# Fifth list tiles of two experts in one stage of TensorE: 96 rows each, on column groups

## The chip, the cores and the metric

The kernel runs on one core of a Trainium2 chip. The metric is the device time of one execution in microseconds (us), the lower the better. All arithmetic is in 32-bit floats (f32). The engines are TensorE (PE, matrix products; its weight loads are listed apart as PEld), VectorE (DVE), ScalarE (ACT), GpSimd (POOL) and SyncE (SP, which issues most plain DMAs).

## The reference

Two layers on 1024 tokens of 1024 channels: group norm, a convolution-attention hybrid and a residual sum; then layer norm, causal attention of 16 heads and a residual sum; then layer norm and a mixture of eight experts with a residual sum. The change lies in the mixture alone:

```python
gate_logits = jax.nn.softmax(x @ gate_w + gate_b, axis=-1)
selected = (gate_logits >= THRESHOLD).astype(x.dtype)          # THRESHOLD = 0.1
weights = gate_logits * selected
weights = weights / jnp.where(wsum == 0, jnp.ones_like(wsum), wsum)   # wsum: sum over experts
for e in range(E):                                             # E = 8
    out = out + weights[:, e:e + 1] * (x @ expert_w[e] + expert_b[e])
```

A token counts for an expert only where its gate is at least 0.1. The reference, run on its inputs, selects 560, 592, 542, 569, 578, 552, 545 and 538 of the 1024 tokens for experts 0 to 7.

## The kernel before

**Lists.** While attention's output is projected, each token's gates are computed, and each expert gets a list of its selected tokens (`place`, `enter`, `read_lists`). The list's entries are read 128 at a time, called list tiles. `gather`, `slot` and `add` hold the token numbers and gates. For experts 1 to 6 five list tiles are always worked off, 640 entries (`SLOTS`, L61). Experts 0 and 7 (`SHORT`, L62) have four, from lists without the last 128 tokens; the last 128 tokens go through these two experts densely (`dense` and `last_pe`). After all this a branch (L1219) handles what longer lists hold; its condition is `most_i > SLOTS`, where `most_i` is the largest list, and for experts 0 and 7 their list plus 128 (`last_lists`, L1006).

**One list tile.** `get` (L1060, through `fetch`) gathers its rows with four indirect DMAs issued by POOL, of 256 channels each. `put` (L1063, through `turn`) transposes them on DVE, so that channels lie on partitions, as TensorE's stationary operand needs. The result is scaled by the gate on ACT and added to the output by an indirect DMA issued by POOL (`add_rows`, L743).

**Four tiles in two pairs.** `products` (L1079) takes two list tiles, 256 rows, against a 1024 x 1024 expert matrix by Strassen's scheme in Winograd's form: seven block products, each of four f32 matmuls with 128 x 128 stationary blocks and 512 moving columns. `row_sums` forms the sums of row blocks (`sums_of_A`, L147), and `first_sum`, `second_sum`, `third_sum` (L1048) and `fourth_sum` form those of the weights. `third_sum` overwrites the block b12 of the expert's weights in place. The seven products alternate between two groups of three PSUM banks (`mm`, `tr`), and DVE takes each out.

**The fifth tile.** `left_over` (L1117) multiplies one list tile by the expert's weights directly: for each of two halves of the columns, eight f32 matmuls of a full 128 x 128 stationary block (`weighted`, L731, the matmul on L737). It stands ahead of the expert's products.

**Order.** From L1152 on the order is written out by hand. For each expert: `left_over` (1 to 6 only), then `load(e + 1)` (the next expert's weights, two DMAs on SP), then `products` for pair 0 and pair 1. Both take a dictionary `between`: other engines' work that is issued after product n of the seven. Weights of even and odd experts have buffers of their own (`w_even`, `w_odd`), so an expert's weights load during the one before it.

Of the kernel before, what the change touches and what calls it, by code (L numbers as in the profile page):

```python
# [28 lines left out]
F32 = mybir.dt.float32  # L32
# [6 lines left out]
P = 128  # L39
# [18 lines left out]
NEG = -1e29  # L58
THRESHOLD = 0.1
Q = 4  # L60
SLOTS = 5 * P  # L61
SHORT = (0, E - 1)  # L62


# [1 line left out]
def kernel(  # L66
# [80 lines left out]
    def sums_of_A(a11, a12, a21, a22, s1, s2, s4):  # L147
        nc.vector.tensor_add(s1, a21, a22)
        nc.vector.tensor_sub(s2, s1, a11)
        nc.vector.tensor_sub(s4, a12, s2)  # L150
        nc.vector.tensor_sub(a21, a11, a21)

    def layer_norm(ln, t, dst):

# [300 lines left out]
    with ExitStack() as attention:  # L455
# [20 lines left out]
        def sums_of_B():  # L476
            nc.vector.tensor_sub(T[0], b12, b11)
            nc.vector.tensor_sub(T[1], b22, T[0])
            nc.vector.tensor_sub(b12, b22, b12)
            nc.vector.tensor_sub(T[2], b21, T[1])  # L480

        n_products = 0
# [221 lines left out]

        return w_tile(f"{name}{e}_{r}", expert_w[e][:, ts(r, HALF)], home=home)

    def expert_bias(e, home, name="w_e"):
        bias = home.tile([P, C], F32, tag="bias", name=f"{name}_bias{e}", bufs=1)
        nc.sync.dma_start(bias, expert_b[e].partition_broadcast(P))
        return bias  # L710

    def fetch(e, k, home, name="w_e", bufs=None):

        row = home.tile([P, Q, C // Q], F32, tag="xg", name=f"{name}_xg{e}_{k}", bufs=bufs)
        for g in range(Q):
            nc.gpsimd.indirect_dma_start(  # L716
                out=row[:, g, :],
                out_offset=None,
                in_=table[: (TOK - P) * Q, :] if e in SHORT else table,
                in_offset=bass.IndirectOffsetOnAxis(ap=gather[:, e, k * Q + g : k * Q + g + 1], axis=0),  # L720
            )
        return row

    def turn(row_T, row):

        nc.vector.transpose(  # L726
            row_T.rearrange("p c (g j) -> p g c j", g=Q),
            row.rearrange("p g (c i) -> p g c i", c=NC),
        )

    def weighted(gate, row_T, w, bias, home, name, between={}):  # L731
# [8 lines left out]
            nc.scalar.mul(y[:, ts(j, HALF)], y[:, ts(j, HALF)], gate)  # L740
        return y

    def add_rows(e, k, y):  # L743
        nc.gpsimd.indirect_dma_start(  # L744
            out=out[: TOK - P, :] if e in SHORT else out,
            out_offset=bass.IndirectOffsetOnAxis(ap=add[:, e, k : k + 1], axis=0),
            in_=y,
            in_offset=None,
            compute_op=ALU.add,
        )  # L750

    def by_rows(e, tiles, w, bias, home, name):

        tiles = list(tiles)

        def turned(k, row):
            row_T = home.tile([P, NC, P], F32, tag="row_T", name=f"{name}_xg_T{e}_{k}", bufs=3)
            turn(row_T, row)
            return row_T

        fetched = [fetch(e, k, home, name) for k in tiles[:2]]
        ready = [turned(tiles[0], fetched[0])]
        for n, k in enumerate(tiles):
            if n + 2 < len(tiles):
                fetched.append(fetch(e, tiles[n + 2], home, name))
            if n + 1 < len(tiles):
                ready.append(turned(tiles[n + 1], fetched[n + 1]))
            add_rows(e, k, weighted(slot[:, e, 1, k : k + 1], ready[n], w, bias, home, f"{name}{e}_{k}"))

    with ExitStack() as gating:  # L770
        l2, l2w = pool(gating, "l2"), pool(gating, "l2w", 2)
# [234 lines left out]
        def last_lists(entries):  # L1006
            read_lists(1, E, entries)


            pn = tr("pn")  # L1010
            nc.tensor.matmul(pn[:, :E], ones, kept, start=True, stop=True)
            need = l2.tile([P, E], F32, tag="need", name="need")
            nc.vector.tensor_copy(need, pn[:, :E])
            pn0 = tr("pn0")
            nc.tensor.matmul(pn0[:, :2], ones, kept_short, start=True, stop=True)
            nc.vector.tensor_scalar(need[:, :: E - 1], pn0[:, :2], float(P), None, ALU.add)
            most = l2.tile([P, 1], F32, tag="most", name="most")
            nc.vector.tensor_reduce(most, need, AX.X, ALU.max)
            nc.vector.tensor_copy(most_i, most)
# [11 lines left out]
        def half(e, j, l):  # L1031
            return w[e][l][:, 4 * j : 4 * j + 4, :]
# [15 lines left out]
        def third_sum(e):  # L1048

            T3[e] = half(e, 0, 1)  # L1050
            if e == E - 1:
                free = w_even.tile([P, NC, HALF], F32, tag="w", name="free")
                T3[e] = free[:, : NC // 2, :]
                last_rows.append(free[:, NC // 2 : NC // 2 + 2, :].rearrange("p a b -> p (a b)"))
            nc.vector.tensor_sub(T3[e], half(e, 1, 1), half(e, 0, 1))

        row = {}
        last = SLOTS // P - 1

        def get(e, k):  # L1060
            row[e, k] = fetch(e, k, two, bufs=3)

        def put(e, k):  # L1063

            if k == last:
                A[e, k] = l2w.tile([P, NC, P], F32, tag="row_T", name=f"one{e}", bufs=3)
                turn(A[e, k], row[e, k])
            else:
                pair, i = divmod(k, 2)
                if i == 0:  # L1070
                    A[e, pair] = two.tile([P, 2, NC, P], F32, tag="A", name=f"A{e}_{pair}")
                turn(A[e, pair][:, i, :, :], row[e, k])
# [6 lines left out]
        def products(e, pair, between):  # L1079
# [34 lines left out]
            rows_out(1, 0)  # L1114
            add_rows(e, 2 * pair + 1, y[1])

        def left_over(e):  # L1117

            between = {0: lambda: (fourth_sum(e), put(e, 1), get(e, 3)), 1: lambda: row_sums(e, 0)}
            get(e, 2)  # L1120
            y = weighted(slot[:, e, 1, last : last + 1], A[e, last], w[e], bias[e], l2w, f"one{e}", between)
            add_rows(e, last, y)

        with tc.manual_schedule():
# [23 lines left out]
            )  # L1150
            get(0, 3)
            for e in range(E):  # L1152
                if e not in SHORT:
                    left_over(e)
                if e + 1 < E:
                    load(e + 1)
# [6 lines left out]
                if e == 0:  # L1163
                    between[2] = lambda: (stage(3, NT - 1), fourth_sum(0), put(0, 2))
                    between[3] = lambda: (entries.append(copy_lists(1)), put(0, 3))
                    between[4] = lambda: (last_lists(entries[0]), row_sums(0, 1))
                    between.pop(1)
                elif e == E - 1:
                    between[0] = lambda: (third_sum(e), get(e, 3))
                    between[1] = lambda: (fourth_sum(e), put(e, 2))  # L1170
                if e + 1 < E - 1:
                    between[5] = lambda: get(e + 1, last)
                    between[6] = lambda: get(e + 1, 0)
                elif e + 1 == E - 1:
                    between[5] = lambda: get(e + 1, 0)
                    between[6] = lambda: get(e + 1, 1)
                products(e, 0, between)
                between = {}
                if e + 1 < E - 1:
                    between = {  # L1180
                        1: lambda: (bias.update({e + 1: expert_bias(e + 1, l2w)}), put(e + 1, last)),
                        2: lambda: (put(e + 1, 0), get(e + 1, 1)),
                        4: lambda: first_sum(e + 1),
                        5: lambda: second_sum(e + 1),
                        6: lambda: bias_step(e + 1),
                    }
                elif e + 1 == E - 1:
                    between = {
                        1: lambda: (bias.update({e + 1: expert_bias(e + 1, l2w)}), put(e + 1, 0), get(e + 1, 2)),
                        2: lambda: put(e + 1, 1),  # L1190
                        3: lambda: row_sums(e + 1, 0),
                        4: lambda: first_sum(e + 1),
                        5: lambda: second_sum(e + 1),
                        6: lambda: bias_step(e + 1),
                    }
                else:
                    between = {
                        1: lambda: nc.sync.dma_start(last_rows[0], out[ts(NT - 1, P), :]),
                        4: lambda: nc.vector.scalar_tensor_tensor(
                            last_rows[0], bias[e], gated[NT - 1][0][:, e, 1:2], last_rows[0], ALU.mult, ALU.add  # L1200
                        ),
                    }
# [16 lines left out]
    with tc.If(count > SLOTS), ExitStack() as rest:  # L1219
        w_rest, l3 = pool(rest, "w_rest", 4), pool(rest, "l3", 3)  # L1220
        for e in range(E):
            w_e = [half_weights(e, r, w_rest, "w_r") for r in range(2)]
            tiles = range(SLOTS // P - 1, NT - 1) if e in SHORT else range(SLOTS // P, NT)
            by_rows(e, tiles, w_e, expert_bias(e, l3, "w_r"), l3, "w_r")


# [57 lines left out]
```

## Time and profile before

| | us |
|---|---|
| median of 3 runs | 1311.58 |
| lowest and highest | 1308.51, 1311.72 |
| the profiled execution | 1310.25 |
| its span, first to last instruction | 1308.4 |
| PE busy | 1286.6 |
| DVE busy | 664.3 |
| POOL busy | 344.3 |
| ACT busy | 245.3 |
| DVE add of 128 x 512 (L1101) | 0.691 |
| DVE transpose of one list tile (L726) | 1.241 |
| POOL gather, one of four of a list tile (L716) | 1.048 |
| DMA of half an expert's weights, issue to landing | 12.1 |

A row of a group reads: source line, engine, operation, what is written <- what is read, shape of the stationary block (partitions x columns, with a star), shape of the output, count | busy time in us, mean ns of one | idle time of the engine before them, and what ended it. A row of the timeline or of the chain begins with the start in us from the span's start and the length in us. Matmul records overlap each other, since the next one enters while the last one leaves; so the distance of starts is what a matmul costs, and not its length. An f32 matmul leaves two records. The line numbers are those of the kernel before.

### The profile page before, as it was taken

To read this page: it belongs to the slowest core of one execution; us is meant where nothing else is said; L and a number is where in the kernel's file an instruction comes from. 1 tells how busy PE (TensorE), PEld (TensorE's weight loads), DVE (VectorE), ACT (ScalarE), POOL (GpSimd) and SP (SyncE) were. 2 spreads that over 40 slices of the span, in tenths; PEclk is the share of its full clock that TensorE was granted. 3 is DMA by queue.
4 is the path that set the end of the run, shared out by engine and by line. 5 is a ranking of instruction groups with operands and counts; after the bars stand their busy time and mean duration, and the time that the engine had idled before them with its cause. 6 is when DMAs were issued, how large, how long until landed. Compare 5 with 4: busy or idle time off the path is not lost.

```text
span 1308.4 us, 12324 instructions
## 1 busy us (share of the span) xinstructions
PE 1286.6 (98%) x4550; PEld 695.5 (53%) x4550; DVE 664.3 (51%) x1250; ACT 245.3 (19%) x572; POOL 344.3 (26%) x365
## 2 busy tenths in 40 slices
PE   9999999998999999999999998999999999999998
PEld 5445894777884555555554544444444444444443
DVE  5874220566323555554444755655646465555642
ACT  3200111330001333333323322111111111110110
POOL 0000060230000211111111113445454544453530
PEclk9999999998999999999999998999999999999999
DMA  9020023512201202010505215374757566555532
GB/s 350 2 65 17 1 76 92 203 65 81 65 18 46 65 1 65 1 65 1 193 17 196 96 65 201 73 220 115 214 124 190 147 164 174 145 165 140 111 75 58
DMA packets 61042, 136.12 MB, mean 104 GB/s; under 512 B 5905, under 2 KB 20257, under 8 KB 60977
## 3 DMA queue, kind: packets, MB, share of 16 engines
q1 hardware_dynamic: 47664, 94.32, 20.7%
q0 software_dynamic: 13312, 40.96, 14.4%
q8 instruction: 38, 0.62, 0.2%
q14 instruction: 28, 0.22, 0.1%
HBM read 97.51 MB, written 33.55 MB: 100 GB/s over the span
## 4 chain that ended last, share of the span: by engine, by line
PE 93%; DVE 4%; POOL 1%; DMA 1%; issue 1%; ACT 0%; DVEq 0%; ACTq 0%; POOLq 0%
PE p L1093 28%; PE pqk L489 15%; PE po L646 8%; PE pq L257 7%; PE pv L489 7%; PE one_pe L737 6%; PE pT L376 3%; PE py L441 2%; PE pk L319 2%; PE pc L340 2%; PE pv L401 2%; PE sc L573 2%; PE pst L617 2%; PE pa L627 2%; PE last_pe L1209 1%; POOL w_e_xg L716 1%
## 5 line engine op out<-in xcount | busy, mean ns | idle before, releaser
L716 POOL DMA_INDIRECT w_e_xg<-rows,gather x152 | 159.2, 1048 | 69.1 <-issue 42.0
L1093 PE MATMUL p<-w_e,A 128*128 128x512 f32 x368 | 164.6, 597 | 1.8 <-DVE slot L954 1.8
L605 POOL TENSOR_TENSOR s<-s,total 128x256 f32<-128x256 f32 x64 | 51.5, 826 | 346.4 <-DVE total L602 338.4
L1093 PEld LDWEIGHTS p<-w_e,A 128*128 128x128 f32 x368 | 70.4, 192 | 90.5 <-issue 88.6
L646 PE MATMUL po<-w_p,y_T 128*128 128x512 f32 x256 | 116.1, 598 | 0.0
L744 POOL DMA_INDIRECT out_dram<-y,add x32 | 60.8, 1899 | 205.7 <-ACT y L1099 133.1
L1093 PE MATMUL p<-T,S 128*128 128x512 f32 x256 | 112.7, 592 | 0.0
L1099 ACT ACTIVATE y<-y,slot 128x512 f32<-128x512 f32 x64 | 46.2, 722 | 341.3 <-DVE y L1107 172.5
L257 PE MATMUL pq<-w_q,xn 128*128 128x512 f32 x224 | 99.6, 596 | 1.4 <-DVE q_s L261 1.1
L489 PE MATMUL pqk<-ln,w_qk 128*128 128x512 f32 x192 | 85.0, 592 | 0.0
L737 PE MATMUL one_pe<-w_e,one 128*128 128x512 f32 x192 | 83.4, 592 | 0.0
L1093 PEld LDWEIGHTS p<-T,S 128*128 128x128 f32 x256 | 48.6, 190 | 60.8 <-issue 60.7
L646 PEld LDWEIGHTS po<-w_p,y_T 128*128 128x128 f32 x256 | 46.3, 190 | 49.1 <-issue 48.7
L257 PEld LDWEIGHTS pq<-w_q,xn 128*128 128x128 f32 x224 | 41.8, 190 | 51.8 <-issue 47.4
L726 DVE STREAM_TRANSPOSE A<-w_e_xg 128x1024 f32<-128x1024 f32 x32 | 39.7, 1241 | 51.4 <-DMA w_e_xg<-rows,gather 51.4
L737 PEld LDWEIGHTS one_pe<-w_e,one 128*128 128x128 f32 x192 | 36.5, 190 | 45.9 <-issue 45.7
L595 ACT ACTIVATE s<-s,top 128x256 f32<-128x256 f32 (+1 forms) x128 | 56.6, 443 | 18.1 <-DVE top L593 18.0
L489 PEld LDWEIGHTS pqk<-ln,w_qk 128*128 128x128 f32 x192 | 35.9, 190 | 42.1 <-issue 41.1
L489 PE MATMUL pqk<-T,S_qk 128*128 128x512 f32 x128 | 57.7, 593 | 0.0
L1093 PE MATMUL p<-w_e,S 128*128 128x512 f32 x128 | 57.5, 592 | 0.0
L1093 PE MATMUL p<-T,A 128*128 128x512 f32 x128 | 57.5, 592 | 0.0
L618 ACT COPY s_T<-pst 128x384 f32<-128x384 f32 x64 | 27.5, 481 | 157.6 <-PE pst L617 157.6
(256 smaller groups left out, 1801.0 us busy)
## 6 DMA issues: line engine op xcount, KB each, us to landing
w_e<-in_expert_w_dram SPq DMA_DIRECT2D x16, 2048.0 KB, 12.1
w_qk<-in_W_attnT_dram SPq DMA_DIRECT2D x8, 1024.0 KB, 6.4
xn<-in_xT_dram SPq DMA_DIRECT2D x8, 512.0 KB, 7.8
x_at<-in_x_dram SPq DMA_DIRECT2D x8, 512.0 KB, 7.1
w_v<-in_W_attnT_dram SPq DMA_DIRECT2D x2, 2048.0 KB, 11.8
x_rows<-x_at SPq DMA_DIRECT2D x8, 512.0 KB, 2.7
w_p<-in_W_projT_dram SPq DMA_DIRECT2D x2, 2048.0 KB, 8.4
xb<-x_rows SPq DMA_DIRECT2D x8, 512.0 KB, 6.8
```

Source lines behind the costliest of these rows:

```text
L257: nc.tensor.matmul(pq, xn[:, c, ts(t, P)], w_q[kc][:, c, :], start=(c == 0), stop=(c == NC - 1))
L376: nc.tensor.matmul(out_T[:, g, :, :], window[:, kc, :, :].rearrange("p i j -> p (i j)"), q0[:, kc, first : first + n_i, nj, :], start=(kc ...
L489: nc.tensor.matmul(bank, stationary(c), moving(c), start=(c == 0), stop=(c == NC // 2 - 1))
L595: nc.scalar.activation(s[:, h, cols], s[:, h, cols], AF.Exp, bias=top[:, qt, h : h + 1], accum_out=total[:, qt, h : h + 1],)
L605: nc.gpsimd.tensor_mul(s[:, :, cols], s[:, :, cols], total[:, qt, :].unsqueeze(2).to_broadcast([P, 2, (qt + 1) * P]),)
L646: nc.tensor.matmul(po, y_T[:, c, ts(t, P)], w_p[j][:, c, :], start=(c == 0), stop=(c == NC - 1))
L716: nc.gpsimd.indirect_dma_start(out=row[:, g, :], out_offset=None, in_=table[: (TOK - P) * Q, :] if e in SHORT else table, in_offset=bass.I ...
L726: nc.vector.transpose(row_T.rearrange("p c (g j) -> p g c j", g=Q), row.rearrange("p g (c i) -> p g c i", c=NC),)
L737: nc.tensor.matmul(pe, row_T[:, c, :], w[j][:, c, :], start=(c == 0), stop=(c == NC - 1))
L744: nc.gpsimd.indirect_dma_start(out=out[: TOK - P, :] if e in SHORT else out, out_offset=bass.IndirectOffsetOnAxis(ap=add[:, e, k : k + 1], ...
L1093: nc.tensor.matmul(bank, a[:, c, :], b[:, c, :], start=(c == 0), stop=(c == NC // 2 - 1))
L1099: nc.scalar.mul(y[i][:, ts(j, HALF)], y[i][:, ts(j, HALF)], slot[:, e, 1, 2 * pair + i : 2 * pair + i + 1])
```

## The change

The fifth tile of experts 1 to 6 holds 96 rows instead of 128 (`LEFT`), so a list may hold 608 entries ahead of the branch. The fifth tiles of two experts, odd d and even e = d + 1, are worked off together, between the products of d and those of e. TensorE's output columns are split in groups. In a first stage, of 24 matmuls for each half of the weights' columns, columns 0 to 63 and 64 to 95 take d's 96 rows, and columns 96 to 127 take rows 64 to 95 of e; each has its own stationary and its own moving operand. In a second stage e's rows 0 to 63 are multiplied on two groups of 64 columns, each with half the contraction, and DVE adds the two halves after ACT has copied one. By the time of the first stage the block b12 of d's weights has been overwritten; with the sign of that sum turned, it holds b12 - b22, and the product comes out right if the rows for b22 are a1 + a2 (`sum_left`). The weights of d are therefore read until that stage ends, and `load(e + 1)` into the same buffers comes after it.

The gathers and transposes of both fifth tiles move into the products of d. Odd experts start without a fifth tile and take over the order that expert 7 had. Biases get two buffers, and their DMA is issued ahead of the second pair's products. A fifth tile's gather is three indirect DMAs.

```diff
-SLOTS = 5 * P
+LEFT = 96
+SLOTS = 4 * P + LEFT
@@ sums_of_A
-        nc.vector.tensor_sub(a21, a11, a21)
+        nc.vector.tensor_sub(a21, a21, a11)
@@ sums_of_B
-            nc.vector.tensor_sub(b12, b22, b12)
+            nc.vector.tensor_sub(b12, b12, b22)
...
-    def fetch(e, k, home, name="w_e", bufs=None):
+    def fetch(e, k, home, name="w_e", bufs=None, slots=P):
...
-        for g in range(Q):
+        for g in range(slots // 32):
...
@@ last_lists
-            nc.vector.tensor_scalar(need[:, :: E - 1], pn0[:, :2], float(P), None, ALU.add)
+            nc.vector.tensor_scalar(need[:, :: E - 1], pn0[:, :2], float(LEFT), None, ALU.add)
@@ third_sum
-            nc.vector.tensor_sub(T3[e], half(e, 1, 1), half(e, 0, 1))
+            nc.vector.tensor_sub(T3[e], half(e, 0, 1), half(e, 1, 1))
...
+        def sum_left(e):
+
+            A[e, "sum"] = l2w.tile([P, NC, P], F32, tag="row_T", name=f"sum{e}", bufs=3)[:, : NC // 2, :LEFT]
+            nc.vector.tensor_add(A[e, "sum"], A[e, last][:, : NC // 2, :LEFT], A[e, last][:, NC // 2 :, :LEFT])
+
         def left_over(e):
 
+            d = e - 1
             between = {0: lambda: (fourth_sum(e), put(e, 1), get(e, 3)), 1: lambda: row_sums(e, 0)}
             get(e, 2)
-            y = weighted(slot[:, e, 1, last : last + 1], A[e, last], w[e], bias[e], l2w, f"one{e}", between)
-            add_rows(e, last, y)
+            y_d, y_e = (l2w.tile([P, C], F32, tag="ye", name=f"left{e}_{i}", bufs=3) for i in range(2))
+
+            for j in range(2):
+                bank = (tr if j else mm)(f"left{e}_{j}")
+                for c in range(NC):
+                    a = A[d, last][:, c, :] if j == 0 or c < NC // 2 else A[d, "sum"][:, c - NC // 2, :]
+                    for lo, hi, stationary, of in (
+                        (0, 64, a[:, :64], d),
+                        (64, LEFT, a[:, 64:LEFT], d),
+                        (LEFT, P, A[e, last][:, c, 64:LEFT], e),
+                    ):
+                        nc.tensor.matmul(
+                            bank[lo:hi, :], stationary, w[of][j][:, c, :], start=(c == 0), stop=(c == NC - 1)
+                        )
+                between[j]()
+                y = y_d[:LEFT, ts(j, HALF)]
+                nc.vector.tensor_add(y, bank[:LEFT, :], bias[d][:LEFT, ts(j, HALF)])
+                nc.scalar.mul(y, y, slot[:LEFT, d, 1, last : last + 1])
+                nc.vector.tensor_add(y_e[64:LEFT, ts(j, HALF)], bank[LEFT:, :], bias[e][LEFT:, ts(j, HALF)])
+            add_rows(d, last, y_d, LEFT)
+
+            for j in range(2):
+                bank = (tr if j else mm)(f"rest{e}_{j}")
+                for c in range(NC // 2):
+                    for i in range(2):
+                        nc.tensor.matmul(
+                            bank[ts(i, 64), :],
+                            A[e, last][:, i * (NC // 2) + c, :64],
+                            w[e][j][:, i * (NC // 2) + c, :],
+                            start=(c == 0),
+                            stop=(c == NC // 2 - 1),
+                        )
+                other = two.tile([P, HALF], F32, tag="U", name=f"other{e}_{j}", bufs=5)
+                nc.scalar.copy(other[:64, :], bank[64:, :])
+                y = y_e[:64, ts(j, HALF)]
+                nc.vector.tensor_add(y, bank[:64, :], bias[e][:64, ts(j, HALF)])
+                nc.vector.tensor_add(y, y, other[:64, :])
+                y = y_e[:LEFT, ts(j, HALF)]
+                nc.scalar.mul(y, y, slot[:LEFT, e, 1, last : last + 1])
+            add_rows(e, last, y_e, LEFT)
@@ the order of the experts
-                if e not in SHORT:
+                if e % 2 == 0 and e:
                     left_over(e)
...
-                elif e == E - 1:
+                elif e % 2:
                     between[0] = lambda: (third_sum(e), get(e, 3))
                     between[1] = lambda: (fourth_sum(e), put(e, 2))
-                if e + 1 < E - 1:
-                    between[5] = lambda: get(e + 1, last)
-                    between[6] = lambda: get(e + 1, 0)
-                elif e + 1 == E - 1:
+                if e % 2 == 0:
                     between[5] = lambda: get(e + 1, 0)
                     between[6] = lambda: get(e + 1, 1)
+                elif e + 1 < E:
+                    between[5] = lambda: (get(e, last), get(e + 1, last))
+                    between[6] = lambda: get(e + 1, 0)
                 products(e, 0, between)
...
+                    bias[e + 1] = expert_bias(e + 1, l2w, tag="xg", bufs=2)
...
+                if e % 2 == 0:
+                    between[1] = lambda: (put(e + 1, 0), get(e + 1, 2))
+                    between[2] = lambda: put(e + 1, 1)
+                    between[3] = lambda: row_sums(e + 1, 0)
+                elif e + 1 < E:
+                    between[1] = lambda: put(e, last)
+                    between[2] = lambda: (put(e + 1, last), sum_left(e))
+                    between[3] = lambda: (put(e + 1, 0), get(e + 1, 1))
```

More of the change, by code (lines that the diff above doesn't have):

```diff
@@ L705, in half_weights, with expert_bias @@
         return w_tile(f"{name}{e}_{r}", expert_w[e][:, ts(r, HALF)], home=home)
-    def expert_bias(e, home, name="w_e"):
-        bias = home.tile([P, C], F32, tag="bias", name=f"{name}_bias{e}", bufs=1)
+    def expert_bias(e, home, name="w_e", tag="bias", bufs=1):
+        bias = home.tile([P, Q, C // Q], F32, tag=tag, name=f"{name}_bias{e}", bufs=bufs).rearrange("p a b -> p (a b)")
         nc.sync.dma_start(bias, expert_b[e].partition_broadcast(P))
         return bias
-    def fetch(e, k, home, name="w_e", bufs=None):
+    def fetch(e, k, home, name="w_e", bufs=None, slots=P):
         row = home.tile([P, Q, C // Q], F32, tag="xg", name=f"{name}_xg{e}_{k}", bufs=bufs)
-        for g in range(Q):
+        for g in range(slots // 32):
             nc.gpsimd.indirect_dma_start(
@@ L722, in fetch, with turn @@
         return row
-    def turn(row_T, row):
+    def turn(row_T, row, slots=P):
         nc.vector.transpose(
-            row_T.rearrange("p c (g j) -> p g c j", g=Q),
-            row.rearrange("p g (c i) -> p g c i", c=NC),
+            row_T[:, :, :slots].rearrange("p c (g j) -> p g c j", j=32),
+            row[:, : slots // 32, :].rearrange("p g (c i) -> p g c i", c=NC),
         )
@@ L741, in weighted, with add_rows @@
         return y
-    def add_rows(e, k, y):
+    def add_rows(e, k, y, slots=P):
         nc.gpsimd.indirect_dma_start(
             out=out[: TOK - P, :] if e in SHORT else out,
-            out_offset=bass.IndirectOffsetOnAxis(ap=add[:, e, k : k + 1], axis=0),
-            in_=y,
+            out_offset=bass.IndirectOffsetOnAxis(ap=add[:slots, e, k : k + 1], axis=0),
+            in_=y[:slots, :],
             in_offset=None,
@@ L754, in by_rows, with gates @@
         tiles = list(tiles)
+        def gates(k):
+            if k > SLOTS // P or e in SHORT:
+                return slot[:, e, 1, k : k + 1]
+            late = home.tile([P, 1], F32, tag="late", name=f"{name}_late{e}")
+            nc.vector.memset(late, 0.0)
+            nc.vector.tensor_copy(late[LEFT:, :], slot[LEFT:, e, 1, k : k + 1])
+            return late
         def turned(k, row):
@@ L767, in by_rows @@
                 ready.append(turned(tiles[n + 1], fetched[n + 1]))
-            add_rows(e, k, weighted(slot[:, e, 1, k : k + 1], ready[n], w, bias, home, f"{name}{e}_{k}"))
+            add_rows(e, k, weighted(gates(k), ready[n], w, bias, home, f"{name}{e}_{k}"))
     with ExitStack() as gating:
@@ L1054, in third_sum @@
                 last_rows.append(free[:, NC // 2 : NC // 2 + 2, :].rearrange("p a b -> p (a b)"))
-            nc.vector.tensor_sub(T3[e], half(e, 1, 1), half(e, 0, 1))
+            nc.vector.tensor_sub(T3[e], half(e, 0, 1), half(e, 1, 1))
         row = {}
-        last = SLOTS // P - 1
+        last = SLOTS // P
         def get(e, k):
-            row[e, k] = fetch(e, k, two, bufs=3)
+            row[e, k] = fetch(e, k, two, bufs=3, slots=LEFT if k == last else P)
         def put(e, k):
@@ L1066, in put @@
                 A[e, k] = l2w.tile([P, NC, P], F32, tag="row_T", name=f"one{e}", bufs=3)
-                turn(A[e, k], row[e, k])
+                turn(A[e, k], row[e, k], LEFT)
             else:
@@ L1167 @@
                     between.pop(1)
-                elif e == E - 1:
+                elif e % 2:
                     between[0] = lambda: (third_sum(e), get(e, 3))
                     between[1] = lambda: (fourth_sum(e), put(e, 2))
-                if e + 1 < E - 1:
-                    between[5] = lambda: get(e + 1, last)
-                    between[6] = lambda: get(e + 1, 0)
-                elif e + 1 == E - 1:
+                if e % 2 == 0:
                     between[5] = lambda: get(e + 1, 0)
                     between[6] = lambda: get(e + 1, 1)
+                elif e + 1 < E:
+                    between[5] = lambda: (get(e, last), get(e + 1, last))
+                    between[6] = lambda: get(e + 1, 0)
                 products(e, 0, between)
-                between = {}
-                if e + 1 < E - 1:
+                if e + 1 < E:
+                    bias[e + 1] = expert_bias(e + 1, l2w, tag="xg", bufs=2)
                     between = {
-                        1: lambda: (bias.update({e + 1: expert_bias(e + 1, l2w)}), put(e + 1, last)),
-                        2: lambda: (put(e + 1, 0), get(e + 1, 1)),
                         4: lambda: first_sum(e + 1),
@@ L1186 @@
                     }
[L1187 to L1195, printed above, removed]
+                if e % 2 == 0:
[6 more added lines that the diff above has]
+                    between[3] = lambda: (put(e + 1, 0), get(e + 1, 1))
                 else:
@@ L1222 @@
             w_e = [half_weights(e, r, w_rest, "w_r") for r in range(2)]
-            tiles = range(SLOTS // P - 1, NT - 1) if e in SHORT else range(SLOTS // P, NT)
+            tiles = range(SLOTS // P, NT - 1 if e in SHORT else NT)
             by_rows(e, tiles, w_e, expert_bias(e, l3, "w_r"), l3, "w_r")
```

## The prediction

> **What bounds the kernel now.** I read the totals first, then the chain that ended last, then one expert's stretch engine by engine, then TensorE's own records.
>
> The page: TensorE (PE) works 98% of the span, no other engine much over half.
>
> ```profile
> span 1308.4 us, 12324 instructions
> PE 1286.6 (98%) x4550; PEld 695.5 (53%) x4550; DVE 664.3 (51%) x1250; ACT 245.3 (19%) x572; POOL 344.3 (26%) x365
> ```
>
> The chain of waits over the experts (start, length, what): the fifth tiles (one_pe) and the products of four tiles (p) follow each other without a gap; experts 6 and 7 (the last row here) run without a fifth tile between them, and without a gap too. A fifth tile costs its whole length.
>
> ```profile
> 869.94 13.73 PE one_pe L737 x32
> 883.67 48.07 PE p L1093 x112
> 931.74 13.73 PE one_pe L737 x32
> ...
> 1192.67 96.13 PE p L1093 x224
> ```
>
> One period of 61.80 us (products and a fifth tile), busy time of PE, PEld, DVE, ACT and POOL, then the clock: only PE is full, and its clock is 1.00.
>
> ```profile
> 883.67:945.47 61.80, 61.80 (x145) 27.36 (x145) 34.03 (x38) 7.22 (x10) 31.77 (x27) 1.00 0.63 169
> ```
>
> So the change is worth what it does to PE's time between two experts. An f32 matmul leaves two records; a fifth tile is 16 matmuls of 512 columns, 32 records: 13.73/32 = 0.429 us a record, 0.858 a matmul, whatever the number of rows used.
>
> **What column groups do here.** PE groups: full array, 64 columns (128x64), full array by 256.
>
> ```profile
> L319 PE MATMUL pk<-w_kv,xn 128*64 128x256 f32 x256 | 27.9, 380 | 0.0
> L489 PE MATMUL pv<-w_v,ln 128*128 128x256 f32 x192 | 43.6, 380 | 0.0
> ```
>
> Records of the same length: 27.9/256 = 0.109 us each in two column groups, 43.6/192 = 0.227 on the full array. Two groups of 64 do run side by side. Four groups of 32 do as well (parts), each with its own moving tile:
>
> ```profile
> 723.73 0.65 PE L852 MATMUL parts<-row_T,gw 128*32 128x128 f32 x16
> 724.30 0.70 PE L646 MATMUL po<-w_p,y_T 128*128 128x512 f32 x1
> ```
>
> 16 records of 128 columns take 0.57 us to the next start; the half of pk's pair, 27.84/128/2 = 0.109 us, times four rounds is 0.435. So four at a time, and 0.135 us over. That rest is the change of size. It shows best here:
>
> ```profile
> 610.89 7.03 PE L489 MATMUL pqk<-ln,w_qk 128*128 128x512 f32 x16
> 617.75 3.60 PE L489 MATMUL pqk<-T,S_qk 128*128 128x512 f32 x8
> 621.28 0.87 PE L627 MATMUL pa<-s_T,v 128*64 128x256 f32 x8
> 622.08 0.92 PE L573 MATMUL sc<-qk 64*128 64x256 f32 x8
> 622.94 0.88 PE L617 MATMUL pst<-ident,s 128*128 128x128 f32 x6
> ```
>
> Start to start, 16 records take 6.86 us, the 8 after them 3.53 instead of 3.43: 0.10 more, because pa has another size. The weight loads say why:
>
> ```profile
> 619.90 0.19 PEld L489 LDWEIGHTS pqk<-T,S_qk 128*128 128x128 f32 x1 [0.24 <-issue]
> 620.33 0.19 PEld L489 LDWEIGHTS pqk<-T,S_qk 128*128 128x128 f32 x1 [0.24 <-issue]
> 621.28 0.63 PEld L627 LDWEIGHTS pa<-s_T,v 128*64 128x64 f32 x8 [0.76 <-issue]
> ```
>
> Loads of one size run a record ahead, every 0.43 us. The first load of another size starts 0.95 us after the one before it, with the first matmul of that size, so after the old matmuls have left. pa then lasts 0.80 us (622.08 - 621.28), where two 256-wide rounds (0.2175) and two 128-wide ones (0.109) make 0.65: 0.15 over. sc (64 rows): 0.86, 0.21 over.
>
> **The change, part by part.**
>
> *Removed, per pair of experts (1-2, 3-4, 5-6):* two fifth tiles, 2 x 13.73 = 27.46 us of PE, all on the path.
>
> *Added, first stage:* 16 steps (8 chunks, 2 column halves) of three f32 matmuls on columns 0-63, 64-95 and 96-127: 96 rows of the first expert, 32 of the second. If all three overlap, a step is 0.858 us. But 64 is followed by 32, 32 and then 64 again: two sizes in every step, 32 changes of size. No row shows 64 beside 32. The nearest are the changes of size above: with each, PE lets the old matmuls finish before it loads the new weights. Against taking them over: in all of these rows the new tile also covers columns of the old one, here it doesn't. For: a new tile of the *same* size on the same columns is loaded ahead freely, so it is the size, not the overlap of columns, that holds the load back. I take the serial reading. A step is then 0.858 + 0.15 (64, priced by pa) and 0.858 + 0.14 (both 32s together, priced by parts), 2.01 us; sixteen are 32.1.
>
> *Added, second stage:* 64 rows of the second expert, contraction split over two groups of 64: 16 f32 matmuls in 8 rounds of 0.858, 6.87, and one change of size 0.15: 7.0 us. Two groups of 64 have a row (pk), so this holds either way.
>
> *Into and out of the full array:* 0.10 (pqk before pa) and 0.10 (po after parts: its first record is 0.70 instead of 0.59).
>
> *Sum:* 32.1 + 7.0 + 0.2 - 27.46 = +11.8 us a pair; three pairs +35.5. The profiled execution took 1310.25 us (span 1308.4 and 1.85 around it), 1.33 under the median of the runs shown: 1310.25 + 35.5 = 1345.8; a median of several runs may lie that 1.33 higher.
>
> *Bounds of the unknown cost:* all overlap: 13.73 + 6.87 + 0.4 = 21.0, -6.5 a pair, -19.4. Serial and changes free: 27.46 + 6.87 + 0.2 = 34.5, +7.1 a pair, +21. Serial and every change as dear as sc's (0.21): 16 x 2.14 + 7.1 + 0.2 = 41.5, +14.1 a pair, +42.
>
> The Trainium skill, "TensorEngine Tiling (Array Packing)", Key Properties, says that a change of tiling mode, not just of tile, drains TensorE; it lists 128x64 and 128x32 as modes of their own. By that rule the sum is the serial one, +35.5 us; by its other rule there, that tiles operate independently, it would be -19.4. The trace's late loads agree with the first and show nothing of 64 beside 32.
>
> *Other engines, costed at nothing.* DVE per pair: 4 adds of 0.69 become 8 no longer than that, plus one sum of chunks under 0.69, less 2 x 0.31 for transposes of 96 rows (from 1.24): +2.8 us against 2 x (61.80 - 34.03) = 55 us idle. ACT: two copies, about 0.5 each as s_T<-pst. POOL: two gathers fewer (38 for 40, one each 1.3), as many scatters. Subtractions with swapped operands (sums_of_A, sums_of_B, third_sum): same count and size. If PE's stage were to shrink by 6.5 us, 48 us of DVE idle would be left.
>
> *Moved.* The six gathers of both fifth tiles and four of the next tile now queue on POOL after product 5 of the odd expert: at 1.28 us each, 13 us, 3 us more than eight. The transpose that waits for the last stalls DVE some 2 us; behind it stand PSUM evictions. PE uses six banks of 3.43 us, so it has four products, 14 us, before it notices. SP: the load of expert e+1 waits for the first stage's last read of the odd expert's weights, later by that stage. Behind it on SP stand its second half and the bias: 2 x 12.1 + 4.2 = 28 us; first_sum wants it 7 + 24 + 17 = 48 us after: 20 us to spare. Odd experts start with no fifth tile before them, as expert 7 does already in the 96.13 row. The chunk sum reads tiles transposed two products earlier.
>
> **Rivals.**
> 1. *All three groups overlap* (faster, 0.15). pk and parts speak for it: groups of one size do. Price -19.4: 1310.25 - 19.4 = 1290.9. It decides where a step is under (27.46 - 7.2)/16 = 1.27 us.
> 2. *Half overlap* (0.02): sizes overlap but every weight load is exposed, or starts queue in the order of issue, three records a step, 3 x 0.429 = 1.29 us: 20.6 + 7.2 = 27.8, +1 us: 1311. parts, four starts at a time, speaks against it.
> 3. *The two 32s don't overlap either* (0.02): a step of 3 x 0.858 + 0.3 = 2.87, 46 + 7.2 = 53.2, +77: 1387. parts speaks against it.
> 4. *The late branch runs.* Lists may hold 608 rows instead of 640. The reference on its inputs fills at most 592, so the branch stays off; I give it nothing.
>
> **How the numbers follow.** Serial, the forecast: 0.81, own range 1310.25 + 21 to + 42, rounded out by the runs' 1.5 us: 1330 to 1354. It leaves out the 0.19 of the rivals, so that is the range. Slower by over 0.3% (about what runs of this kernel can tell from no change): 0.81 + 0.02 = 0.83. Faster: 0.15. Within: 0.02.
>
> **What would show it.** Serial: PE's chain shows about 32 us for the first stage and 7.0 for the second at each of three pairs; starts of 64-column records lie 2.0 us apart, from step to step, and the loads of 32 columns start only after the 64's matmuls. Overlapping: about 13.9 and 7.0, three starts within a few hundredths. The p rows should stay at 48.07 an expert with no DVE or POOL wait on PE; a PE wait for A, S or w_e would break the cover above. A step at 1.3 us or less makes the prediction wrong in sign.

## The result, and the profile after

| | before | changed kernel |
|---|---|---|
| median, us | 1311.03 (4 runs) | 1343.65 (4 runs) |
| lowest and highest | 1308.51, 1311.72 | 1342.67, 1345.26 |
| the profiled execution, and its span | 1310.25, 1308.4 | 1343.69, 1341.8 |

The changed kernel takes 1.0254 of the time before, with a 95% interval of 1.0236 to 1.0271: it is slower by some 33 us. The forecast was 1345.8, with a range of 1330 to 1354.

The totals of the changed kernel: TensorE is busy for 33 us more and still for 98% of the span; the other engines hardly moved.

```profile
span 1341.8 us, 12710 instructions
PE 1319.5 (98%) x4742; PEld 680.7 (51%) x4742; DVE 670.6 (50%) x1265; ACT 248.5 (19%) x578; POOL 336.0 (25%) x359
```

Its chain of waits, over one pair of experts (start, length, what). The first stage is `left`, the second `rest`; the products `p` of two experts follow.

```profile
916.40 31.76 PE left L1148 x96
948.16 7.02 PE rest L1162 x32
955.17 96.33 PE p L1103 x224
1051.51 31.76 PE left L1148 x96
```

A row of this chain begins where the one before it ends (916.40, while the first record of 64 columns starts at 916.33), so it holds the change of size into its first matmuls. 31.76 + 7.02 = 38.78 us stand where two fifth tiles took 2 x 13.73 = 27.46. All three pairs show the same lengths. The products of two experts take 96.33 us instead of the 96.13 of experts 6 and 7 before: 0.20 for the change back into the full array.

The timeline of the weight loads in that first stage says what fills the 31.76:

```profile
915.38 0.19 PEld L1103 LDWEIGHTS p<-T,A 128*128 128x128 f32 x1 [0.24 <-issue]
916.33 0.19 PEld L1148 LDWEIGHTS left<-w_e,one 128*64 128x64 f32 x2 [0.76 <-DVE T L1046]
917.33 0.14 PEld L1148 LDWEIGHTS left<-w_e,one 128*32 128x32 f32 x4 [0.81 <-issue]
918.31 0.19 PEld L1148 LDWEIGHTS left<-w_e,one 128*64 128x64 f32 x2 [0.84 <-issue]
919.31 0.14 PEld L1148 LDWEIGHTS left<-w_e,one 128*32 128x32 f32 x4 [0.81 <-issue]
```

The loads come in turn: two for 64 columns (an f32 matmul has two), 1.00 us later four for 32 columns (two groups together), 0.98 us later the next 64. A step is 1.98 us. While one size works, nothing of the other size is loaded, although the columns are others.

### The profile page after: what moved, and what is told of

It reads as the page before. It is cut to its first block, busy times and chain, and to the rows that moved or that the text cites. A ratio compares the mean times of both kernels' runs of the same rounds, so it can differ in the third digit from the quotient of the medians.

```text
span 1341.8 us, 12710 instructions
## 1 busy us (share of the span) xinstructions
PE 1319.5 (98%) x4742; PEld 680.7 (51%) x4742; DVE 670.6 (50%) x1265; ACT 248.5 (19%) x578; POOL 336.0 (25%) x359
## 4 chain that ended last, share of the span: by engine, by line
PE 93%; DVE 4%; POOL 1%; issue 1%; DMA 1%; ACT 0%; DVEq 0%; ACTq 0%; POOLq 0%
PE p L1103 28%; PE pqk L491 14%; PE po L648 8%; PE left L1148 7%; PE pq L259 7%; PE pv L491 6%; PE pT L378 3%; PE py L443 2%; PE pk L321 2%; PE pc L342 2%; PE pv L403 2%; PE sc L575 2%; PE pst L619 2%; PE pa L629 2%; PE rest L1162 2%; PE last_pe L1260 1%
## 5 line engine op out<-in xcount | busy, mean ns | idle before, releaser
L718 POOL DMA_INDIRECT w_e_xg<-rows,gather x146 | 154.8, 1060 | 66.1 <-issue 42.0
L746 POOL DMA_INDIRECT out_dram<-y,add x32 | 57.9, 1809 | 188.0 <-ACT y L1109 124.6
L1148 PE MATMUL left<-w_e,one 128*32 128x512 f32 (+1 forms) x240 | 84.2, 609 | 0.0
L1148 PEld LDWEIGHTS left<-w_e,one 128*32 128x32 f32 (+1 forms) x240 | 13.7, 116 | 59.1 <-issue 57.6
```

Source lines behind the costliest of these rows:

```text
L718: nc.gpsimd.indirect_dma_start(out=row[:, g, :], out_offset=None, in_=table[: (TOK - P) * Q, :] if e in SHORT else table, in_offset=bass.I ...
L746: nc.gpsimd.indirect_dma_start(out=out[: TOK - P, :] if e in SHORT else out, out_offset=bass.IndirectOffsetOnAxis(ap=add[:slots, e, k : k ...
L1148: nc.tensor.matmul(bank[lo:hi, :], stationary, w[of][j][:, c, :], start=(c == 0), stop=(c == NC - 1))
```

## The experiments

Theory S: at each change between groups of 64 and of 32 columns TensorE finishes the old size before it loads the new one, so a 64 never runs beside a 32. Rivals: M, f32 matmuls with 512 columns and moving tiles of their own overlap no more than two at a time; O, the new order of gathers, biases and loads costs the time; W, a group of 64 with 512 columns keeps all others out.

**All groups of 32.** The first expert's 96 rows on three groups instead of two.

```diff
-                        (0, 64, a[:, :64], d),
+                        (0, 32, a[:, :32], d),
+                        (32, 64, a[:, 32:64], d),
                         (64, LEFT, a[:, 64:LEFT], d),
```

Expected:

> First stage in four groups of 32 columns (the first expert's 96 rows on three of them), so no change of size inside it; all else as in the changed kernel. Theory S (with each change between 64 and 32 columns TensorE finishes the old size before it loads the new one, so 64 never runs beside 32): 16 steps of 0.858 us, 13.7 us a pair for 31.76; the pair costs 13.7 + 7.0 + 0.2 = 20.9 for 27.46 before the change, -6.5 us, three pairs -19.5: 1291.5 us, faster than both kernels. Rival M (f32 matmuls of 512 columns with moving tiles of their own don't overlap more than two at a time): 2 x 0.858 a step, 27.5 + 7.2 a pair, +7.2 us, about 1333. Rival O (the new order of gathers, biases and loads costs the time): no faster than 1340.

Measured: 1289.68 us, against 1309.43 for the kernel before on the same chip, a ratio of 0.9853 (0.9837 to 0.987). It is the fastest of the kernels here. Its chain, and its weight loads:

```profile
916.34 13.87 PE left L1149 x128
930.21 7.02 PE rest L1163 x32
937.23 96.33 PE p L1103 x224
```

```profile
916.27 0.16 PEld L1149 LDWEIGHTS left<-w_e,one 128*32 128x32 f32 x8 [0.76 <-DVE y L1117]
916.73 0.13 PEld L1149 LDWEIGHTS left<-w_e,one 128*32 128x32 f32 x4 [0.30 <-issue]
917.15 0.13 PEld L1149 LDWEIGHTS left<-w_e,one 128*32 128x32 f32 x4 [0.30 <-issue]
```

There is one more matmul a step, and the step falls from 1.98 to 0.87 us: four loads go out together every 0.43 us, each a round ahead. Rivals M and O fall with this run alone, since it has four moving streams and the new order.

**The same matmuls, sorted by size.** In each half of the columns first the eight of 64 columns, then the sixteen of 32.

```diff
+                for sizes in ((0,), (1, 2)):
-                for c in range(NC):
+                    for c in range(NC):
...
-                    for lo, hi, stationary, of in (
+                        for lo, hi, stationary, of in (groups[n] for n in sizes):
```

Expected:

> The same matmuls as the changed kernel's, in another order: in each half of the columns first the eight of 64 columns, then the sixteen of 32. Four changes of size in the first stage and into the second for 32. Theory S: streams of 2 x 0.858 a step remain, the price of a change, (31.76 - 16 x 1.717)/32 = 0.134 us, goes 28 times a pair: -3.8 us a pair, -11.3 us: 1332.4 us; the first stage takes 28.0 us. Rivals M and O, in which a change of size has no price: 1343.7 us as the changed kernel.

Measured: 1333.2 us, and 28.00 us for the first stage.

```profile
919.07 28.00 PE left L1150 x96
947.07 7.02 PE rest L1164 x32
```

Sixteen steps of 2 x 0.858 are 27.47; 0.53 us is left for four changes. So the 33 us of loss have two parts: the sizes' running one after the other, which stays here, and the price of the changes, which went. This run prices the changes; it doesn't test the overlap, since in this order a 64 stands next to a 32 at the changes alone.

**Every second step in reverse order.** One change of size a step instead of two.

```diff
-                    for lo, hi, stationary, of in (
...
+                    for lo, hi, stationary, of in groups if c % 2 == 0 else groups[::-1]:
```

Expected:

> Every second step in reverse order (64, 32, 32, then 32, 32, 64): one change of size a step instead of two, 16 fewer a pair. Theory S: -16 x 0.134 = -2.1 us a pair, -6.4 us: 1337.2 us, first stage 29.6 us. Rivals M and O: 1343.7 us.

Measured: 1337.28 us. From 916.72 to 946.47, in the rows of the chain, the first stage takes 29.75 us, 29.75 - 27.47 = 2.28 more than without changes. Such a row holds the change into the first group and, here, 16 inside the stage: 17, at 0.134 us each. (None is left between the stages, and the second takes 6.87 us.) Counted in this way the run sorted by size has 4 and the changed kernel 32, and 4, 17 and 32 changes all give 0.13 us a change: the price goes by their number.

**The new order without column groups.** Both fifth tiles on the full array, one after the other, and no second stage; everything that was moved stays moved.

```diff
-                    for lo, hi, stationary, of in (
...
+                for bank, of in zip(banks, (d, e)):
+                    for c in range(NC):
+                        a = A[of, last][:, c, :]
...
+                        nc.tensor.matmul(
+                            bank[:LEFT, :], a[:, :LEFT], w[of][j][:, c, :], start=(c == 0), stop=(c == NC - 1)
+                        )
```

Expected:

> The new order of gathers, loads, biases and experts, but both fifth tiles on the full array, 96 columns each, one after the other; no second stage, no copy of halves. Theory S: TensorE's time is that of the kernel before, 2 x 13.73 us a pair, and the rest is hidden: 1311 us. Rival O: the order itself costs, 1320 us or more, up to 1343.

Measured: 1309.55 us, against 1309.43 before, a ratio of 1.0001 (0.9992 to 1.0011).

```profile
916.26 27.47 PE left L1146 x64
943.73 96.13 PE p L1103 x224
```

27.47 us a pair is the time of two fifth tiles before; a stationary block of 96 columns costs what one of 128 does. The moved gathers, transposes, loads and biases cost nothing that can be measured. Rival O is out.

**Two groups of 64.** Columns 64 to 127 take rows 32 to 95 of the first expert.

```diff
-                        (64, LEFT, a[:, 64:LEFT], d),
-                        (LEFT, P, A[e, last][:, c, 64:LEFT], e),
+                        (64, P, a[:, 32:LEFT], d),
```

Expected:

> The first stage in two groups of 64: columns 64 to 127 take rows 32 to 95 of the first expert; the second expert's rows 64 to 95 are left out, so a quarter of the array's work is done twice for the wrong rows. Groups of 64 and of 512 columns, but of one size. Theory S: they overlap, 0.858 us a step, first stage 13.7 us, time about 1291. Rival W (a group of 64 with 512 moving columns keeps others out, whatever their size): 2 x 0.858 a step, first stage 27.5 us, time about 1331.

Measured, in one run: 1291.59 us, first stage 13.88, that is 16 x 0.858 = 13.73 and 0.15 for the change into the first group. So a 64 does run beside another 64 at 512 columns, and rival W is out. With the all-32 kernel, that leaves the difference in size as what keeps 64 and 32 apart.

```profile
918.94 13.88 PE left L1147 x64
932.83 6.87 PE rest L1161 x32
```

The second stage, which follows in the same size here, takes 6.87 instead of 7.02: the one change between the stages, 0.15 us.

**The second stage in groups of 32 too.** From the all-32 kernel:

```diff
-                    for i in range(2):
+                    for i in range(4):
                         nc.tensor.matmul(
-                            bank[ts(i, 64), :],
-                            A[e, last][:, i * (NC // 2) + c, :64],
-                            w[e][j][:, i * (NC // 2) + c, :],
+                            bank[ts(i, 32), :],
+                            A[e, last][:, i // 2 * (NC // 2) + c, ts(i % 2, 32)],
+                            w[e][j][:, i // 2 * (NC // 2) + c, :],
```

Expected:

> The all-32 kernel, and its second stage in groups of 32 too: two groups of the second expert's rows 0-31 and 32-63, each for both halves of the contraction, eight rounds as before. So no change of size is left between the two stages. Theory S: one change less at each of three pairs, 3 x 0.134 = 0.4 us under the all-32 kernel: 1289.3 us, a difference that this measurement can hardly tell from none. If rounds of four groups were dearer than rounds of two, it would show in the second stage, 7.0 us now.

Measured: 1300.19 us (1294.94 to 1302.58), a ratio of 0.992 (0.9904 to 0.9936) to the kernel before: a miss, some 10 us more than the all-32 kernel, where 0.4 less was expected. The chain over the second pair:

```profile
1037.03 13.87 PE left L1149 x128
1050.90 5.62 PE rest L1163 x45
1056.52 0.39 issue
1056.91 1.05 PE rest L1163 x4
1057.96 0.39 issue
1058.36 0.59 PE rest L1163
1058.94 0.12 issue
1059.07 2.63 PE rest L1163 x14
1061.70 96.33 PE p L1103 x224
```

The first stage runs as it should. In the second, after 128 + 45 records (43 rounds of four), TensorE stands still again and again and waits for nothing that the profile shows ("issue"). The stage takes 10.8 us (1061.70 - 1050.90), in the third pair 10.65 and in the first 8.0, instead of 7.02: 8.4 us together. The other 2 us come ahead of the first pair, where nothing was edited: its first stage starts at 918.3 instead of 916.3. Other kernels here show as much (919.07 in the run sorted by size), so it needn't belong to the edit.

**What the late starts are.** Two kernels, run once each: the all-32 kernel with the first stage issued twice over (64 rounds in a row), once with all four groups and once with three. The first one's edit of the all-32 kernel:

```diff
-                for c in range(NC):
+                for n, c in enumerate((*range(NC), *range(NC))):
...
-                            bank[lo:hi, :], stationary, w[of][j][:, c, :], start=(c == 0), stop=(c == NC - 1)
+                            bank[lo:hi, :], stationary, w[of][j][:, c, :], start=(n == 0), stop=(n == 2 * NC - 1)
```

Expected, with four groups:

> The all-32 kernel (second stage in groups of 64) with the first stage's matmuls issued twice over into the same sums, so the fifth tiles' products come out doubled: 64 rounds of four groups in a row instead of 32. In the run whose second stage was in groups of 32 too, rounds of four went on for 48, and starts came late from the 42nd to 47th on, with TensorE waiting for nothing but issue. Theory I (instructions reach TensorE more slowly than the eight that a round of four groups uses up in 0.429 us, and a lead of instructions lasts some 43 rounds): late starts here too from about round 43, in the first stage; the stage takes 32 us or more instead of 2 x 13.8 = 27.6, the time is 1345 or more. Rival R (two groups that read the same moving chunk at once, as in that run's second stage, hinder each other): no late starts, 27.6 us, 1289.7 + 3 x 13.8 = 1331.

Expected, with three:

> The same with three groups of 32 instead of four: the second expert's rows 64 to 95 are left out, and the first stage is issued twice over. Six instructions a round of 0.429 us (72 ns each) instead of eight (54 ns). Theory I, with a supply between 54 and 72 ns an instruction: no late starts in 64 rounds, 27.6 us, time about 1331. With a supply slower than 72 ns: late starts, later than with four groups. Rival R: no late starts.

Measured with four groups: 1337.99 us. The chain over the second pair:

```profile
1049.13 19.22 PE left L1149 x170
1068.35 0.36 issue
1068.70 1.31 PE left L1149 x5
1070.02 0.12 issue
1070.14 9.19 PE left L1149 x81
```

Measured with three groups: 1331.24 us, and 27.60 us for the stage, without a break:

```profile
916.72 27.60 PE left L1148 x192
```

The late starts come back in the first stage: TensorE first stands still after 208, 170 and 164 records in the three pairs, that is 52, 42 and 41 rounds of four. So they don't belong to the second stage's operands. With three groups, which all read the same moving chunk, late starts never come in 64 rounds, and rival R is out. That is what a supply of instructions between 54 ns (eight a round of 0.429 us) and 72 ns (six a round) apiece would do, with a lead that lasts some 40 to 50 rounds. But theory I's size was wrong: the stage takes 28.8, 30.2 and 30.0 us and not 32 or more, because after 1.2 to 2.6 us lost in late starts full rounds go on to the end. That a supply of instructions lies behind it is argued from these two runs; no row of the profile shows it, and why the second stage in groups of 32 did not recover as fast stays open. The run with three groups also shows that three groups as such don't hold each other back: 27.60/32 = 0.86 us a step with one size, where 64 + 32 + 32 took 1.98.

## Why the prediction was right, point by point

**The step that decided, 64 and 32 in turn.** The forecast priced the two sizes one after the other, from rows in which the new tile also covered the old one's columns, and said that this had to be carried over to groups side by side. It held: a step took 1.98 us for 2.01 forecast. The runs with one size alone (0.87 us a step with four groups of 32, 0.87 with two of 64, 0.86 with three of 32) show that it is the size, and the runs with 4 and 17 changes show what each change adds to 16 x 2 x 0.858 us. The Trainium skill, "TensorEngine Tiling (Array Packing)", Key Properties, says that a change of tiling mode drains TensorE, and these runs agree: 0.13 to 0.14 us a change, and no overlap across it.

**The price of a change.** Forecast 0.15 for the 64s (from pa) and 0.14 for the 32s (from parts); measured (31.76 - 27.47)/32 = 0.134 on the mean. 32 changes at some 0.01 too much are the 0.3 us between 32.1 and 31.76.

**The second stage:** forecast 7.0, measured 7.02. **Into and out of the full array:** forecast 0.2, a late start of 0.10 and a first record 0.10 longer; measured 0.20 in the products' row.

**The sum.** Forecast +11.8 us a pair; measured 38.78 + 0.20 - 27.46 = 11.52, three pairs 34.6. The span grew by 33.4. The rest lies outside the pairs: the products begin at 835.50 us instead of 837.10, after stretches in which the change only swaps operands, and what follows the last product takes 0.5 longer. Both are within what runs of one kernel differ by (3 us before). So of the 2.1 us between the forecast and the profiled execution 0.9 is the price of the changes, and the other 1.2, outside the pairs, can be chance.

**The cover of what was moved.** One size was wrong, without harm. I forecast that DVE would stall some 2 us for the last of the ten gathers. The timeline of DVE in the first pair has 6.1, 1.8 and 3.3 us of waiting for the ten gathers, 11.2 together, and ahead of these 8.6 us of waiting for the expert's own fourth tile, where the kernel before waited 3.04:

```profile
887.32 1.25 DVE L728 STREAM_TRANSPOSE A<-w_e_xg 128x1024 f32<-128x1024 f32 x1 [8.59 <-DMA w_e_xg<-rows,gather]
...
902.63 0.98 DVE L728 STREAM_TRANSPOSE one<-w_e_xg 128x768 f32<-128x768 f32 x1 [6.11 <-DMA w_e_xg<-rows,gather]
903.53 0.65 DVE L1112 TENSOR_TENSOR y<-p,U 128x512 f32<-128x512 f32 x1
905.97 0.98 DVE L728 STREAM_TRANSPOSE one<-w_e_xg 128x768 f32<-128x768 f32 x1 [1.78 <-DMA w_e_xg<-rows,gather]
...
911.28 1.25 DVE L728 STREAM_TRANSPOSE A<-w_e_xg 128x1024 f32<-128x1024 f32 x1 [3.29 <-DMA w_e_xg<-rows,gather]
```

```profile
893.75 0.72 ACT L1109 ACTIVATE y<-y,slot 128x512 f32<-128x512 f32 x1 [14.27 <-DVE y L1117]
894.75 1.84 POOL L746 DMA_INDIRECT out_dram<-y,add  x1 [9.35 <-ACT y L1109]
896.90 0.99 POOL L718 DMA_INDIRECT w_e_xg<-rows,gather  x1 [0.30 <-issue]
```

I had taken the gathers' start from the products' fifth bank and left out that the scatter ahead of them on POOL first waits for ACT, and ACT for DVE, which the 8.6 us had made late: they begin at 896.90. The bias's DMA, too, was sized too small: 11.1 us from issue to landing (median) where 4.2 was assumed. The six PSUM banks and the time to spare covered all this, as forecast: the longest waits of TensorE are those ahead of the experts, and the row of the products has no more than before (1.8 us for slot, once, in both).

```profile
PE row_pt L828 <- DVE row L846: 4.9, 2, 3.7
PE pv L491 <- DVE T L480: 3.5, 1, 3.5
PE p L1103 <- DVE slot L964: 1.8, 1, 1.8
```

DVE's eight evictions took 0.68 to 0.70 us each, the chunk sum 0.52, and a transpose of 96 rows 0.98 for the 0.93 assumed.

**The rivals.** That all three groups overlap was given -19.4 us. It is what the kernel with four groups of 32 shows: 1289.68 - 1309.43 = -19.75. The mechanism was right, for one size of group; the change chose two. The late branch stayed off, as its condition on the lists says.

## What to carry to other kernels

In these runs (f32, 512 moving columns) matmuls on column groups ran side by side only where the groups had one size: split 96 + 32 columns as four of 32, not as 64 + 32 + 32, at least for stages of 32 rounds as here (the next section says why). Before trusting a packing, look at a place in the trace where the size changes: if the first weight load of the new size comes after the old matmuls instead of a record ahead, a mix of sizes runs one size after the other, and pays for every change. Where sizes must be mixed, sort by size: that took the first stage from 31.76 to 28.00 us with the same matmuls.

## What the runs showed of the hardware that was not expected

Four column groups of f32 matmuls with 512 columns, each with its own weight load, kept full pace for some 40 to 50 rounds of 0.429 us, and then TensorE stood still for tenths of a us at a time with nothing to wait for that the profile shows; three groups kept it for 64 rounds. The cause stays open. A stage of 48 rounds of four groups was thereby slower (10.8 us for the part that took 7.02 on two groups of 64) although no size changed in it. The all-32 kernel stays below this with 32 rounds, after which two groups of 64 follow, at four instructions a round.
